# A Fourier layer's cosine transforms: cosines as the matmul's weights, in eighths of the array, with the modes turned by VectorE

## The chip, the cores and the metric

The kernel runs on one core of a Trainium2 chip. The metric is the device time of one execution in microseconds; the time before is the median of three runs. TensorE (PE) does the matmuls, VectorE (DVE), ScalarE (ACT) and GpSimd (POOL) the rest, and nearly all DMAs are issued from SyncE's queue (SP). PEld is TensorE's weight load, which overlaps its matmuls. PSUM has eight banks of 512 fp32 per partition here: four for attention (tag `pa`), four for the convolution (tag `pc`).

## What is computed

The input x is 32 images of 56 x 56 pixels with 128 channels, all fp32. Two residual layers follow each other:

```python
x = x + window_attention(group_norm(x))     # windows of 7 x 7, shifted by 3, 4 heads
x = x + fourier_block(group_norm(x))
```

The part that matters here is the second one. `N_MODES` is 32.

```python
def _forward_fourier(x, w0, w1):
    x = jnp.transpose(x, (0, 3, 1, 2))                      # b, channel, h, w
    x_fty = dct(x, norm='ortho', axis=-1)                   # along the width
    out_y = jnp.einsum('bixy,ioy->boxy', x_fty[..., :N_MODES], w0)
    xy = idct(out_y padded with zeros, norm='ortho', axis=-1)
    # the same along the height, with w1, gives xx
    return transpose_back(xx + xy)

def _feedforward(x, W1, b1, W2, b2):                        # 128 -> 512 -> 128
    return jax.nn.relu(x @ W1 + b1) @ W2 + b2
```

`fourier_block` is the feed-forward of `_forward_fourier`. So each line of 56 pixels becomes 32 cosine modes for each channel, each mode is mixed over the channels by its own 128 x 128 matrix, and the modes are turned back into 56 pixels.

## The kernel before

**Cycles.** The program goes through cycles; cycle n computes row n of windows (eight rows of windows per image, 256 in all). A row's attention is spread over several cycles: queries, keys and scores in its own cycle (`attn_qk`, L455 for the scores, L463 adds the bias, L473 takes the maximum), the exponential at its end, the division by the sum in the next (`attn_divide`, L499 on POOL), the transpose of the probabilities in the one after (`attn_transpose`, L509), then the values (`attn_values`, L524) and the projection (`attn_project`) three cycles later. L573 adds the residual to the projection and so makes the layer's output `x1`; L590 to L598 take its sums and squares for the next group norm.

**The convolution of an image** starts 11 cycles after its first row (`CONV_BEGIN`) and runs for 16 cycles, numbered c = 0 to 15, next to the attention of the images after. So the c = 8 to 15 of one image fall together with the c = 0 to 7 of the next, and "c = 2" below means both 2 and 10. In c = 0 the width is transformed, in c = 1 and 2 the height, in c = 3 the height's modes are mixed, in c = 4 and 5 the width's; the way back (`modes_back`, L743) is in c = 5 to 8, and the feed-forward in seven parts in c = 8, 9, 10, 12, 13, 14 and 15 (`ff_in`, L780, and `ff_out`, L815; its matmuls are recorded at L110, the helper `halved`).

**Order.** On PE, ACT, DVE and POOL the instructions are issued in the order in which the program is written: `halves_first`, then `eighths` (the values), `quarters` (the scores, and the way back), `attn_max`, `behind_max`, `halves_last`. The names tell what part of TensorE's array the matmuls use: halves are two tiles of 128 rows by 64 columns, quarters four of 64 by 64, eighths eight of 64 by 32. Each engine waits, in its own order, for what its next instruction needs.

**The transform** (`transform`, L670) takes two rows of pixels at a time: `tok` has 112 partitions (row parity r, then the 56 places) and 128 channels. The tokens are the weights, the cosines are the moving operand, block-diagonal for the two rows:

```python
py[hs, c * 2 * NM : (c + 1) * 2 * NM], lhsT=tok[:, c, hs], rhs=dct_sb     # L670: 64 channels by 64 columns
```

The result has the channels on the partitions, as the mixing needs. ScalarE copies it out (L678), scaled by the group norm's 1/std and reordered so that each mode's 56 lines lie side by side, and adds the shift to mode 0 (L685). For the width `tok` is `x1` in SBUF; for the height it is read back from a DRAM copy `scr` in the other order (`load_columns`, tile `htok`). The mixing (`mix`, L704) takes `y[:, k * S : k * S + JP]` as weights, 64 neighbouring numbers.

**Other names.** `load_tokens` and `chunks_of` load x again for the residual (tile `xr`), `add_bias` (L124) adds the projection's bias on POOL. `turn_quarter` (L312 to L323) and `row_stats` (L333) prepare the next image's attention. `load_back` fetches the mixed modes (tile `zT`), `load_quarter` the next image (tile `xin`).

Of the kernel before, what the change touches and what calls it, by code (L numbers as in the profile page):

```python
# [15 lines left out]
S = 56  # L16
# [20 lines left out]
HALVES = (slice(0, P // 2), slice(P // 2, P))  # L37
SQRT_S = float(np.sqrt(float(S)))
# [8 lines left out]
def swin_fourier_kernel(  # L47
# [41 lines left out]
    def chunks_of(t, b, n0, n1):  # L89

        tok = t[b].rearrange("h w c -> (h w) c")
        wrap = (S - SS) // 2
        if n0 < wrap:
            e = min(n1, wrap)
            part = tok[SS * S + n0 * TC : SS * S + e * TC].rearrange("(n p) c -> p n c", p=TC)
            yield n0, e, slice(0, TC), part
        if n0 <= wrap < n1:
            yield wrap, wrap + 1, slice(0, S), t[b, S - 1].unsqueeze(1)
            yield wrap, wrap + 1, slice(S, TC), t[b, 0].unsqueeze(1)
        if n1 > wrap + 1:  # L100
            a = max(n0, wrap + 1)
            t0 = (2 * a + SS) % S * S
            part = tok[t0 : t0 + (n1 - a) * TC].rearrange("(n p) c -> p n c", p=TC)
            yield a, n1, slice(0, TC), part
# [8 lines left out]
    def load_tokens(im, i):  # L113

        n0, n1 = WS * i // 2, WS * (i + 1) // 2
        t = work.tile([TC, 4, C], F32, tag="xr", name="xr", bufs=2)
        for a, e, p, src in chunks_of(x, im.b, n0, n1):
            nc.sync.dma_start(t[p, a - n0 : e - n0], src)
        im.xr[i] = t

    def add_bias(im, i):
        n = WS * (i + 1) // 2 - WS * i // 2
        piece = im.xr[i][:, :n]
        nc.gpsimd.tensor_tensor(  # L124
            piece, piece, bproj.unsqueeze(1).to_broadcast([TC, n, C]), ALU.add
        )

    HW = S // 2

    def load_quarter(b, k, u):  # L130

        if b:
            t = work.tile([P, HW, KB], F32, tag="xin", name="xin", bufs=1)
        elif u:
            t = others[k]
        else:
            t = big.tile([P, NM * S + JP - S], F32, tag="y", name="xin_first", bufs=2)
            t = t[:, : S * KB].rearrange("p (w c) -> p w c", w=S)
            others.append(t[:, HW:])
            t = t[:, :HW]  # L140
        rows = slice(k * (S - KB), k * (S - KB) + KB)
        for cb in range(C // KB):
            cs = slice(cb * KB, (cb + 1) * KB)
            queue = nc.scalar if b == 0 and cb % 2 else nc.sync
            queue.dma_start(t[cs], x[b, rows, u * HW : (u + 1) * HW, cs])
        return t
# [5 lines left out]
    x1 = big.tile([TC, NCH, C], F32, tag="x1", name="x1")  # L152
# [12 lines left out]
    bproj = const_load([TC, C], b_proj.partition_broadcast(TC), "bproj")  # L165
# [49 lines left out]
    dct_w = const_load([TC, 2 * NM], dct, "dct_w")  # L215
    dct_h = const.tile([TC, 2 * NM], F32, tag="dct_h", name="dct_h")
    for r in range(0, TC, S):
        nc.sync.dma_start(dct_h[r : r + S - SS], dct[r + SS : r + S])
        nc.sync.dma_start(dct_h[r + S - SS : r + S], dct[r : r + SS])
# [41 lines left out]
    gmean = const.tile([TC, P], F32, tag="gmean", name="gmean")  # L261
    nc.gpsimd.memset(gmean, 1.0 / (4 * NT))
# [29 lines left out]
    def image_begin(b):  # L292
        im = Image()
        im.b = b
        im.half, im.xw, im.xr, im.eT = {}, {}, {}, {}
        return im
# [215 lines left out]
    def attn_values(im, i, r):  # L512
# [19 lines left out]
        if i % 2 == 0:  # L532
            im.oT = work.tile([P, 2 * RT], F32, tag="oT", name="oT")
# [24 lines left out]
    def attn_project(im, i):  # L558

        if i == 0:  # L560
            im.scr = dram.tile([S, S, C], F32, tag="scr", name="scr", bufs=2)
        oT = im.oT
        n0, n1 = WS * i // 2, WS * (i + 1) // 2
        base = i // 2 * WS
        pp = attn_bank()
        for n in range(n0, n1):
            halved(
                pp[:TC, (n - n0) * C : (n - n0 + 1) * C],
                oT[:, (n - base) * TC : (n - base + 1) * TC],
                wproj,  # L570
            )
        piece = x1[:, n0:n1]
        nc.vector.tensor_tensor(  # L573
            piece,
            pp[:TC, : (n1 - n0) * C].rearrange("p (n c) -> p n c", c=C),
            im.xr[i][:, : n1 - n0],
            ALU.add,
        )
        nc.sync.dma_start(
            im.scr[2 * n0 : 2 * n1].rearrange("(n r) w c -> (r w) n c", r=2), piece  # L580
        )

    def attn_sums(im, i):

        n0, n1 = WS * i // 2, WS * (i + 1) // 2
        piece = x1[:, n0:n1]
        if i == 0:
            im.part = small.tile([TC, NWR, 2, C // 4], F32, tag="part", name="part", bufs=1)
            im.tot = small.tile([TC, 2, C // 4], F32, tag="tot", name="tot")
        nc.vector.tensor_reduce(  # L590
            im.part[:, i, 0],
            piece.rearrange("p n (g c) -> p g n c", c=4),
            axis=AX.XY,
            op=ALU.add,
        )
        sq = im.xr.pop(i)[:, : n1 - n0]
        nc.scalar.activation(sq, piece, AF.Square)  # L597
        nc.vector.tensor_reduce(  # L598
            im.part[:, i, 1],
            sq.rearrange("p n (g c) -> p g n c", c=4),  # L600
            axis=AX.XY,
            op=ALU.add,
        )


    def add_sums(im, i):
        if i:
            nc.gpsimd.tensor_tensor(
                im.tot, im.part[:, 0] if i == 1 else im.tot, im.part[:, i], ALU.add
            )  # L610

    def fourier_stats(im):
        pg = attn_bank()

        for k, t in enumerate((im.tot, im.part[:, NWR - 1])):
# [36 lines left out]
    def transform(im, width, g):  # L652

        if g == 0:
            y = big.tile([P, NM * S + JP - S], F32, tag="y", name="y", bufs=2)
            nc.gpsimd.memset(y[:, NM * S :], 0.0)
            if width:
                im.yw = y
            else:
                im.yh = y  # L660
        y = im.yw if width else im.yh
        if width:
            tok = x1[:, CH * g : CH * (g + 1)]
        else:
            tok = im.cols.pop(g)
        dct_sb = dct_w if width else dct_h
        py = conv_bank()
        for c in range(CH):
            for hs in HALVES:
                nc.tensor.matmul(  # L670
                    py[hs, c * 2 * NM : (c + 1) * 2 * NM],
                    lhsT=tok[:, c, hs],
                    rhs=dct_sb,
                    start=True,
                    stop=True,
                )
        y = y[:, : NM * S].rearrange("p (k s) -> p k s", s=S)
        nc.scalar.mul(  # L678
            y[:, :, 2 * CH * g : 2 * CH * (g + 1)].rearrange("p k (n r) -> p k n r", r=2),
            py[:, : 2 * CH * NM].rearrange("p (n k r) -> p k n r", k=NM, r=2),  # L680
            im.rstd,
        )
        if g == NCH // CH - 1:

            nc.scalar.activation(y[:, 0], y[:, 0], AF.Identity, bias=im.shift)  # L685

    def load_columns(im, g):

        t = work.tile([TC, CH, C], F32, tag="htok", name="htok", bufs=2)
        src = im.scr.rearrange("h (n r) c -> r h n c", r=2)  # L690
        for r in range(2):
            nc.sync.dma_start(t[r * S : (r + 1) * S], src[r, :, CH * g : CH * (g + 1)])
        im.cols[g] = t

    def mix(im, width, g):

        y, wmix = (im.yw, w0sb) if width else (im.yh, w1sb)
# [3 lines left out]
        for c in range(4):  # L701
            for u in range(2):
# [3 lines left out]
                    lhsT=y[:, k * S : k * S + JP],  # L706
# [229 lines left out]
    def half_columns(cycle, rest=False):  # L936
        for im, c in fourier(cycle):
            if rest and c != 3:
                continue
            if c == 0:  # L940
                next(im.stats, None)
                for g in range(4):
                    transform(im, True, g)
            elif c in (1, 2):
                for g in (2 * c - 2, 2 * c - 1):
                    transform(im, False, g)
                    if c == 1:
                        load_columns(im, g + 2)
# [3 lines left out]
            elif c in (4, 5):  # L952
                for g in (2 * c - 8, 2 * c - 7):
                    mix(im, True, g)

# [15 lines left out]
    def eighths(cycle):  # L971
        im, i = row(cycle - 3)
        if im:
            attn_values(im, i, cycle - 3)

# [8 lines left out]
    def next_steps(cycle):  # L984
# [4 lines left out]
            4: ((1, 0), (0, 1, 2)),  # L989
            5: ((1, 1), (3, 4, 5)),  # L990
# [16 lines left out]
    def halves_last(cycle):  # L1007
# [8 lines left out]
        load_first(cycle)  # L1016
        if cycle % NWR == NWR - 1:
            norm_step(cycle)
        if row(cycle)[0]:
            attn_exp(cycle)  # L1020
        im, j = row(cycle - 3)
# [58 lines left out]
    with tc.manual_schedule(engines={ET.PE, ET.Activation, ET.DVE, ET.Pool}):  # L1080
# [11 lines left out]
        extra = big.tile([P, NM * S + JP - S], F32, tag="y", name="a_extra", bufs=2)  # L1092
        extra = extra[:, : NH * NP * WT].rearrange("p (t w j) -> p t w j", t=NH, w=NP)
        a_sb.append(extra)
        for cycle in range(NB * NWR + CONV_BEGIN + FF_AT[-1] - NWR + 1):
# [4 lines left out]
            if not row(cycle - 3)[0]:  # L1100
                behind_max(cycle)
                half_columns(cycle)
                half_columns(cycle, True)
                load_first(cycle)
# [8 lines left out]
            if row(cycle)[0]:  # L1113
                attn_max(cycle)
            behind_max(cycle)
            halves_last(cycle)
# [62 lines left out]
```

## Time and profile before

| | before |
|---|---|
| median of 3 runs | 3375.59 us (3375.02 to 3377.16) |
| profiled execution, its own time | 3375.47 us |
| span of its profile | 3373.7 us |
| granted clock, mean | 0.991 |
| L670, width (`dct_w`): 3584 matmul records, mean | 117.7 us busy, 224 ns |
| L670, height (`dct_h`): 3584 matmul records, mean | 116.3 us busy, 222 ns |
| L704, mixing: 4096 matmul records | 124.9 + 122.8 us busy |
| L678, scaling on ACT: 256, mean | 167.5 us busy, 658 ns |

The page is one profiled execution. Busy times of one engine's groups can overlap on PE, where neighbouring tiles of the array run at the same time, so for PE the time from the start of one group to the start of the next tells more. Each fp32 matmul of the program leaves two records. The first number of a timeline row is its start in the span, the second its length in microseconds. "Idle before" is the engine's idle time, followed by what ended it; "issue" is idle time with no cause in the profile.

### The profile page before, as it was taken

To read this page: it belongs to the slowest core of one execution; us is meant where nothing else is said; L and a number is where in the kernel's file an instruction comes from. 1 tells how busy PE (TensorE), PEld (TensorE's weight loads), DVE (VectorE), ACT (ScalarE), POOL (GpSimd) and SP (SyncE) were. 2 spreads that over 40 slices of the span, in tenths; PEclk is the share of its full clock that TensorE was granted. 3 is DMA by queue.
4 is the path that set the end of the run, shared out by engine and by line. 5 is a ranking of instruction groups with operands and counts; after the bars stand their busy time and mean duration, and the time that the engine had idled before them with its cause. 6 is when DMAs were issued, how large, how long until landed. Compare 5 with 4: busy or idle time off the path is not lost.

```text
span 3373.7 us, 158286 instructions
## 1 busy us (share of the span) xinstructions
PE 3250.4 (96%) x69504; PEld 2559.6 (76%) x69504; DVE 2475.1 (73%) x4873; ACT 1979.3 (59%) x3649; POOL 2337.2 (69%) x2663
## 2 busy tenths in 40 slices
PE   4689999999999999999999999999999999999999
PEld 3567777777777777777787777777777777777776
DVE  7777777777777778777777777778777778777641
ACT  3456666555665566655666665666666666665553
POOL 6777777667767677777677676677777777677641
PEclk8899999999999999999999999999999999999999
DMA  5555555555555556556555555555555556555443
GB/s 101 115 128 137 141 137 137 128 132 141 136 132 134 131 140 148 134 132 140 134 140 143 130 131 135 134 137 138 139 133 137 136 137 149 132 133 138 110 130 100
DMA packets 1157657, 448.86 MB, mean 133 GB/s; under 512 B 509470, under 2 KB 1127104, under 8 KB 1156968
## 3 DMA queue, kind: packets, MB, share of 16 engines
q1 hardware_dynamic: 1148648, 437.34, 54.4%
q8 instruction: 546, 8.95, 1.2%
q10 hardware_dynamic: 7712, 1.24, 0.3%
q14 instruction: 143, 1.17, 0.1%
q0 software_dynamic: 608, 0.17, 0.0%
HBM read 277.01 MB, written 161.48 MB: 130 GB/s over the span
## 4 chain that ended last, share of the span: by engine, by line
PE 79%; DVE 7%; POOL 5%; ACT 4%; issue 3%; DMA 1%; SPq 0%; POOLq 0%; ACTq 0%; DVEq 0%
PE pc L110 36%; PE pa L110 13%; PE pa L433 6%; PE pc L670 5%; PE pc L743 5%; PE pa L455 5%; PE pa L524 4%; PE pc L704 4%; POOL blocks L499 4%; ACT hid L780 2%; POOL a L474 1%; DVE a L463 1%; DVE st L333 1%; DVE eT L509 1%; ACT k L420 1%
## 5 line engine op out<-in xcount | busy, mean ns | idle before, releaser
L499 POOL TENSOR_TENSOR blocks<-a,rs 128x512 f32<-128x512 f32 x1518 | 1289.2, 856 | 639.1 <-DVE rs L487 537.4
L110 PE MATMUL pc<-wff,hid 128*64 128x128 f32 x12544 | 744.2, 273 | 4.5 <-issue 3.2
L110 PE MATMUL pc<-xf,wff 128*64 128x512 f32 (+2 forms) x3584 | 720.2, 539 | 1.0 <-DVE xf L754 0.7
L110 PEld LDWEIGHTS pc<-wff,hid 128*64 128x64 f32 x12544 | 704.9, 137 | 13.3 <-issue 6.1
L110 PEld LDWEIGHTS pc<-xf,wff 128*64 128x64 f32 x3584 | 291.7, 136 | 343.7 <-issue 230.5
L474 POOL TENSOR_TENSOR a<-a,mx 128x784 f32<-128x784 f32 x253 | 381.5, 1508 | 241.8 <-DVE mx L473 208.6
L780 ACT ACTIVATE hid<-pc,b1sb 128x512 f32<-128x512 f32 (+2 forms) x896 | 513.0, 646 | 60.7 <-PE pc L110 52.3
L597 ACT ACTIVATE xr<-x 112x384 f32<-112x384 f32 (+1 forms) x256 | 147.1, 574 | 511.6 <-DVE x L573 511.6
L554 DVE TENSOR_SCALAR oT<-pa,bqkv 128x147 f32<-128x147 f32 (+2 forms) x768 | 171.0, 278 | 373.8 <-PE pa L524 373.8
L110 PE MATMUL pa<-xw,wn 128*64 128x392 f32 x2048 | 401.8, 501 | 29.0 <-ACT wn L389 28.8
L815 DVE TENSOR_TENSOR res<-pc,res 128x512 f32<-128x512 f32 (+3 forms) x257 | 142.9, 566 | 377.5 <-issue 169.5
L440 ACT COPY v<-pa 128x512 f32<-128x512 f32 x256 | 152.2, 595 | 366.0 <-PE pa L433 366.0
L787 POOL TENSOR_TENSOR res<-res,b2sb 128x512 f32<-128x512 f32 (+2 forms) x256 | 266.7, 1048 | 88.2 <-DMA res<-scr 88.1
L420 ACT ACTIVATE k<-pa,bqkv,heads 128x392 f32<-128x392 f32 x512 | 317.4, 673 | 1.6 <-PE pa L110 1.1
L509 DVE STREAM_TRANSPOSE eT<-blocks 128x1024 f32<-128x1024 f32 x256 | 315.6, 1233 | 1.6 <-POOL blocks L499 1.6
L124 POOL TENSOR_TENSOR xr<-xr,bproj 112x384 f32<-112x384 f32 (+1 forms) x256 | 292.3, 1142 | 14.9 <-DMA xr<-in_x_dram 14.7
L480 ACT ACTIVATE a<-a 128x784 f32<-128x784 f32 x253 | 216.2, 855 | 147.1 <-POOL a L474 146.2
L433 PE MATMUL pa<-wn,xw 128*64 128x128 f32 x4096 | 289.2, 282 | 12.0 <-issue 8.7
L463 DVE TENSOR_TENSOR a<-pa,bm 128x392 f32<-128x392 f32 x506 | 262.3, 560 | 35.8 <-PE pa L455 9.7
L524 PEld LDWEIGHTS pa<-eT,v 49*32 49x32 f32 x16384 | 173.3, 105 | 151.5 <-issue 97.0
L110 PE MATMUL pa<-wproj,oT 128*48 128x128 f32 (+1 forms) x3584 | 253.4, 276 | 18.5 <-DVE oT L554 17.3
L433 PEld LDWEIGHTS pa<-wn,xw 128*64 128x64 f32 x4096 | 225.1, 139 | 49.2 <-issue 11.1
(103 smaller groups left out, 5073.4 us busy)
## 6 DMA issues: line engine op xcount, KB each, us to landing
zscr<-z SPq DMA_DIRECT2D x512, 112.0 KB
xin<-in_x_dram SPq DMA_DIRECT2D x496, 112.0 KB
htok<-scr SPq DMA_DIRECT2D x256, 196.0 KB
zT<-zscr SPq DMA_DIRECT2D x192, 256.0 KB
res<-scr SPq DMA_DIRECT2D x160, 256.0 KB
out_dram<-res SPq DMA_DIRECT2D x160, 256.0 KB
scr<-x SPq DMA_DIRECT2D x128, 224.0 KB
xr<-in_x_dram SPq DMA_DIRECT2D x128, 168.0 KB
```

Source lines behind the costliest of these rows:

```text
L110: nc.tensor.matmul(dst[ps], lhsT=lhsT[:, ps], rhs=rhs, start=start, stop=stop)
L124: nc.gpsimd.tensor_tensor(piece, piece, bproj.unsqueeze(1).to_broadcast([TC, n, C]), ALU.add)
L420: nc.scalar.activation(k_sb[:, u], pk[:, :RT].rearrange("p (w j) -> p w j", j=WT), AF.Identity, bias=im.bias[:, 3 + u : 4 + u], scale=head ...
L433: nc.tensor.matmul(pv[HALVES[w % 2], w // 2 * C : (w // 2 + 1) * C], lhsT=im.half[i // NP][:, t0 : t0 + JP], rhs=im.w[:, 2 * C : 3 * C], s ...
L463: nc.vector.tensor_tensor(a[:, 2 * hp : 2 * hp + 2, :, 0:WT].rearrange("p u w j -> p w u j"), ps[hp][:, :RT].rearrange("p (w u j) -> p w u ...
L474: nc.gpsimd.tensor_tensor(a3, a3, mx.unsqueeze(2).to_broadcast([P, 2 * NWR, WT]), ALU.subtract)
L480: nc.scalar.activation(a2, a2, AF.Exp)
L499: nc.gpsimd.tensor_tensor(dst[to, k, :, :n], a3[src, :, kb * KB : kb * KB + n], rs[src].unsqueeze(2).to_broadcast([src.stop - src.start, 2 ...
L509: nc.vector.transpose(eT.rearrange("p t (k j) -> p k t j", k=2), blocks[r % 2])
L524: nc.tensor.matmul(po4[u][h * HD : (h + 1) * HD, pr], lhsT=v[ks, pr, h * HD : (h + 1) * HD], rhs=eT[ks, h * NP + pr, :WT], start=True, sto ...
L780: nc.scalar.activation(hf[:, :n], ph[:, :n], AF.Relu, bias=b1sb[:, f : f + 1])
L787: nc.gpsimd.tensor_tensor(im.res[:m, c0:c1], im.res[:m, c0:c1], b2sb[:m].unsqueeze(1).to_broadcast([m, c1 - c0, C]), ALU.add,)
```

## The change

The operands of the transform change places. The cosines become the weights (56 rows by 32 modes), the pixels the moving operand, and each matmul uses an eighth of the array: the two rows of a pair lie on partitions 0 to 55 and 64 to 119 (`LINE`), and four blocks of 32 channels go to four column blocks. The modes then come out on the partitions, 32 for each block of channels, and VectorE turns each 32 x 32 block on its way out of PSUM (`turn_modes`), which puts the channels on the partitions. ScalarE scales and shifts in SBUF, in place (`scale_modes`). `y` is one tile for both directions, in the order line, mode, so that the mixing's weights are 64 numbers with a step of 32.

```diff
+LINE = (slice(0, S), slice(JP, JP + S))
...
-    def transform(im, width, g):
...
-        for c in range(CH):
-            for hs in HALVES:
-                nc.tensor.matmul(
-                    py[hs, c * 2 * NM : (c + 1) * 2 * NM],
-                    lhsT=tok[:, c, hs],
-                    rhs=dct_sb,
...
-        nc.scalar.mul(
-            y[:, :, 2 * CH * g : 2 * CH * (g + 1)].rearrange("p k (n r) -> p k n r", r=2),
-            py[:, : 2 * CH * NM].rearrange("p (n k r) -> p k n r", k=NM, r=2),
-            im.rstd,
-        )
+    def transform(im, width, h):
+
         if width:
-            tok = x1[:, CH * g : CH * (g + 1)]
+            toks = [x1[:, 2 * CH * h : 2 * CH * (h + 1)]]
         else:
+            toks = [im.cols.pop(2 * h + j) for j in range(2)]
+        dct_sb = (dct_w if width else dct_h)[:, :, 0]
+        py = [conv_bank(), conv_bank()]
+        at = 0
+        for tok in toks:
+            n = tok.shape[1] * KB
+            for g in range(C // KB):
+                cs = slice(g * KB, (g + 1) * KB)
+                for r, ps in enumerate(LINE):
+                    nc.tensor.matmul(
+                        py[r][cs, at : at + n],
+                        lhsT=dct_sb[ps],
+                        rhs=tok[ps, :, cs],
+                        start=True,
+                        stop=True,
+                    )
+            at += n
+        im.py[width, h] = py
+
+    def turn_modes(im, width, h):
+
+        y = y_of[width].rearrange("p (h n r k) -> p h r n k", h=2, r=2, k=NM)[:, h]
+        for r, p in enumerate(im.py.pop((width, h))):
+            nc.vector.transpose(y[:, r], p[:, : 2 * CH * KB])
+
+    def scale_modes(im, width, h):
+
+        y = y_of[width].rearrange("p (h s k) -> p h s k", h=2, k=NM)[:, h]
+        nc.scalar.mul(y, y, im.rstd)
+        nc.scalar.activation(y[:, :, 0], y[:, :, 0], AF.Identity, bias=im.shift)
...
+        y = y_all[:, width * NM * S :][:, : NM * JP].rearrange("p (l k) -> p k l", k=NM)
...
-                    lhsT=y[:, k * S : k * S + JP],
+                    lhsT=y[:, k],
```

So that both rows start on partitions 0 and 64, `x1`, `xr`, `htok` and the projection's output get 128 partitions (8 of each 64 unused; the group norm's sums weigh them with 0), and the loads of `xr` and the stores to `scr` are issued for each row of a pair by itself:

```diff
-        nc.sync.dma_start(
-            im.scr[2 * n0 : 2 * n1].rearrange("(n r) w c -> (r w) n c", r=2), piece
-        )
+        dst = im.scr[2 * n0 : 2 * n1].rearrange("(n r) w c -> r w n c", r=2)
+        for r, ps in enumerate(LINE):
+            nc.sync.dma_start(dst[r], piece[ps])
```

Some steps move. The first half of the width's transform goes into c = 5 of the image before. The height's transforms go from the end of c = 1 and 2 to directly behind the values, in `eighths`; VectorE turns them behind `attn_max`, ahead of the transpose of the probabilities. The scaling follows `attn_exp`. The loads of `htok` are issued ahead of `halves_last`. Three of the next image's row statistics go from c = 1 and 2 (two and one) to c = 0:

```diff
             if c == 0:
                 next(im.stats, None)
-                for g in range(4):
-                    transform(im, True, g)
-            elif c in (1, 2):
-                for g in (2 * c - 2, 2 * c - 1):
-                    transform(im, False, g)
-                    if c == 1:
-                        load_columns(im, g + 2)
+                for h in range(int(im.b > 0), 2):
+                    transform(im, True, h)
+                    turn_modes(im, True, h)
...
+                if c == 5 and im.b + 1 < NB:
+                    transform(images[im.b + 1], True, 0)
+                    turn_modes(images[im.b + 1], True, 0)
...
+        for im, c in fourier(cycle):
+            if c == 1:
+                scale_modes(im, True, 1)
+            if c in (1, 2):
+                transform(im, False, c - 1)
+                if c == 1:
+                    for g in range(2):
+                        load_columns(im, g + 2)
+
+    def columns_turn(cycle):
+        for im, c in fourier(cycle):
+            if c in (1, 2):
+                turn_modes(im, False, c - 1)
+
+    def first_scale(cycle):
+        for im, c in fourier(cycle):
+            if c == 0:
+                scale_modes(im, True, 0)
+            elif c in (1, 2):
+                scale_modes(im, False, c - 1)
...
-            4: ((1, 0), (0, 1, 2)),
-            5: ((1, 1), (3, 4, 5)),
+            3: (None, (0, 1, 2)),
+            4: ((1, 0), (3,)),
+            5: ((1, 1), (4, 5)),
```

## The prediction

> **What bounds the kernel now.** I read the page first: its busy shares, then its chain by engine. Both name TensorE.
>
> ```profile
> PE 3250.4 (96%) x69504; PEld 2559.6 (76%) x69504; DVE 2475.1 (73%) x4873; ACT 1979.3 (59%) x3649; POOL 2337.2 (69%) x2663
> ...
> PE 79%; DVE 7%; POOL 5%; ACT 4%; issue 3%; DMA 1%; SPq 0%; POOLq 0%; ACTq 0%; DVEq 0%
> ```
>
> An average hides which cycle has room, so next came the table by stretches of one image in mid-run. A cycle is one row of windows; c is (cycle - 11) modulo 8. Each stretch runs from the attention values (L524) of a cycle to those of the next.
>
> ```profile
> 1342.60:1359.30 16.70, 16.43 (x376) 13.59 (x372) 10.28 (x22) 10.59 (x19) 11.05 (x13) 1.00 0.47 116
> 1359.30:1372.70 13.40, 13.40 (x273) 9.87 (x273) 10.50 (x20) 7.82 (x13) 8.75 (x11) 1.00 0.64 132
> 1372.70:1384.20 11.50, 11.50 (x293) 10.37 (x294) 10.14 (x19) 6.53 (x13) 7.79 (x9) 1.00 0.49 122
> 1384.20:1394.10 9.90, 9.90 (x186) 6.46 (x184) 8.29 (x17) 6.93 (x13) 8.49 (x11) 1.00 0.52 146
> ```
>
> These are c = 0 to 3: length, then busy time of PE, PEld, DVE, ACT and POOL, then the granted clock. PE fills each, at full clock. But in c = 2 VectorE works 10.14 of 11.50, and the change takes PE work out there and puts VectorE work in. So I followed c = 2 in order of time, by engine. The scores (L455) run on PE from 1373.44 to 1374.24; then VectorE:
>
> ```profile
> 1374.38 1.04 DVE L463 TENSOR_TENSOR a<-pa,bm 128x392 f32<-128x392 f32 x2
> 1375.45 0.97 DVE L473 TENSOR_REDUCE mx<-a 128x16 f32<-128x784 f32 x1
> 1376.34 1.23 DVE L509 STREAM_TRANSPOSE eT<-blocks 128x1024 f32<-128x1024 f32 x1
> 1377.50 1.09 DVE L312 STREAM_TRANSPOSE xw<-xin 128x512 f32<-128x512 f32 x1
> 1378.43 0.88 DVE L317 STREAM_TRANSPOSE xw<-xin 128x384 f32<-128x384 f32 x1
> 1379.17 0.26 DVE L323 COPY xw<-xw 128x168 f32<-128x168 f32 x1
> 1379.35 1.49 DVE L333 BATCH_NORM_STATS2 st<-xw 128x6 f32<-128x392 f32 x3
> 1380.76 0.66 DVE L815 TENSOR_TENSOR res<-pc,res 128x512 f32<-128x512 f32 x1
> 1381.35 0.54 DVE L573 TENSOR_TENSOR x<-pa,xr 112x384 f32<-112x384 f32 x1
> ```
>
> No pause from end to end. Then ScalarE, which stood idle 2.97 us for L573:
>
> ```profile
> 1381.92 0.52 ACT L597 ACTIVATE xr<-x 112x384 f32<-112x384 f32 x1 [2.97 <-DVE x L573]
> 1382.35 0.57 ACT L410 ACTIVATE q<-pa,bqkv 128x392 f32<-128x392 f32 x1
> 1382.82 1.24 ACT L420 ACTIVATE k<-pa,bqkv,heads 128x392 f32<-128x392 f32 x2
> ```
>
> k ends at 1384.06, and the next scores, which need it, start at 1384.90. So a second chain, VectorE to ScalarE to scores, lies 0.84 us under PE's. Over the trace's images k ends 0.85 us before the scores of c = 3 on average, 2.42 in c = 2, 2.67 in c = 1. That is all that PE can give up there.
>
> **The change part by part, for one image.**
>
> *PE, removed.* These are PE's rows in c = 2:
>
> ```profile
> 1375.20 1.80 PE L670 MATMUL pc<-dct_h,htok 112*64 112x64 f32 x56
> 1376.83 3.67 PE L110 MATMUL pc<-wff,hid 128*64 128x128 f32 x64
> ```
>
> From start to start 56 records take 1.63 us: 58.2 ns for two, which run side by side. L670's 7168 records are 112 such pairs an image: 6.52 us, 3.26 of it in c = 0, 1.63 in c = 1 and in c = 2.
>
> *PE, added.* The 64 records of L110 last to 1380.32: 109 ns a pair of 128 columns, 0.85 ns a column. L743 has four tiles side by side at that rate. The new form has eight (rows from 0 and 64, four column blocks). Its nearest row is L524, 49*32: 64 records in 0.74 us, and within that, eight records start in 44 ns, 0.9 ns a column; elsewhere in it they start more slowly, being short. With 448 or 224 columns eight records take 0.38 or 0.19 us. Width has 32 records an image, 1.51 us; height 64, 1.51; together 3.02. If four at once were the limit, 6.04. I take eight, by L524.
>
> *PE, changes of tile form.* From 64-row to 128-row tiles a step costs 0.1 us (L455's last record to L433's first 0.17, between L455's own sets 0.06). The height halves follow L524, which has their form: nothing. The width halves stand between 128-row groups, one in c = 0 and one in c = 5: four steps, 0.4.
>
> Relief: 6.52 - 3.02 - 0.4 = 3.1 us, 99 over 32 images.
>
> *VectorE, added.* Eight transposes of 128x448 out of PSUM. The rows on both sides:
>
> ```profile
> L509 DVE STREAM_TRANSPOSE eT<-blocks 128x1024 f32<-128x1024 f32 x256 | 315.6, 1233 | 1.6 <-POOL blocks L499 1.6
> ...
> L312 DVE STREAM_TRANSPOSE xw<-xin 128x512 f32<-128x512 f32 x124 | 137.0, 1105 | 0.7 <-DMA xin<-in_x_dram 0.7
> ```
>
> With L360 (32 columns, 212 ns), L509 gives 1.03 ns a column; it writes runs of 32. L312 scatters its columns 28 bytes apart: 1.83. The new ones write runs of 32: 0.64 us, of which some 0.08 lies beside the next instruction; two make 1.15 (by L312, 1.9).
>
> *VectorE, moved.* Three statistics (L333, 0.47 apart) go into c = 0, two out of c = 1, one out of c = 2. In c = 0 VectorE idles 4.12 us before L815; PE coming 2.3 earlier leaves 1.8 for 1.4 + 1.15, so L815 starts 0.75 late, out of the 2.67 of room in c = 1.
>
> *The wait in c = 3.* From the last score of c = 2 to k of c = 3 is 10.06 us on average, and becomes 10.06 + 1.15 - 0.47 = 10.75. PE reaches these scores after 10.90 now and after 10.90 - 1.63 = 9.27 then. Wait 1.5. On PE the scores, L433 and all that follows queue behind it.
>
> *The wait in c = 2.* The transform there now follows L524 and takes the two PSUM banks that this cycle's first two L780 free. k ends 10.28 + 1.15 - 0.93 = 10.50 after the scores of c = 1, the second L780 1.15 later, 11.65. PE is there at 10.95 (11.96 to L524 now, less 1.63, plus 0.62). Wait 0.7.
>
> *The wait in c = 0.* The width half wants two banks at once, those of the first two L754. The second ends at 1346.89; PE would come at 1346.5. Wait 0.4; today L670's first group covers it.
>
> *c = 5.* PE gets 0.95 more work, VectorE 1.15; k of c = 6 has 1.13 to spare: nothing.
>
> *The mixing weights.* L704's 64 columns come to lie 128 bytes apart. No strided weight load is in this trace. 32 columns load in 105 ns (L524), 64 in 137, so about 1 ns a column, 62 a load, under 109 for the pair of matmuls. By L312's 1.83 a load takes 113: 4 ns too long, 64 times, 0.25 us an image, 8 in all, which I take as the nearest strided row. Bounds: nothing, and, at a factor of 3, 186 ns, 4.9 us an image. [...]
>
> *ScalarE.* Eight L678 of 0.66 and two L685 go, 5.9 us; four scalings of 128x896 (0.95 by L480, 0.86 for 784) and four small ones of 0.3 come, 5.0. They stand before L597, in ScalarE's pause of 2.97. Nothing; without that pause 1.25 in c = 1 and c = 2.
>
> *DMA.* Stores to scr and loads of xr come in two halves, 17 more issues an image on SP at 0.3 to 0.57 us, 7 us over 101, where SP issues for 2.5 to 7.4 us of each 10 to 17. The loads of htok move ahead of zT's and xin's and wait for the last scr store alone. Nothing; a late xr would show as POOL idle at L124 (14.7 us now).
>
> *Gaps.* L670 has 14.8 us of idle time before its records, mostly "issue". Fewer, longer matmuls should lose half: -7 (0 to -15).
>
> Sum: -99 + 31 x (1.5 + 0.7 + 0.4) + 8 - 7 = -17 us. From the profiled execution's 3375.47 that is 3358.5; the median of the runs, 3375.59, stands 0.1 higher: 3358.6.
>
> **Rivals.**
> A: the second chain is not late, because it has slack I don't see. -99 - 7: 3269. Against it: VectorE's rows follow without a pause.
> B, slower: the turns cost what L312 costs, 0.75 more a pair, in the waits of c = 2 and c = 3: 46 us, 3405. For it: they read PSUM, which no transpose does now. It decides from 0.27 a pair (17 / 62).
> C, slower: strided weights at a third of the rate, (4.9 - 0.25) x 32 = 149, 3507. It decides from 0.8 us an image, a factor of 2.
> D: the eighths run four at once, so the change does not do what it says: 97 more, 3455.
>
> **How the numbers follow.** Forecast 0.50, its own range 3335 to 3380 (turns 0.15 a pair either way, 9; weights 0 to 16; gaps 0 to 15; no wait in c = 0, 12). A 0.13, B 0.17, C 0.08, D 0.06; waits in cycles taken as free 0.06, up to 3430. 3268 to 3430 leaves out C, D and a little more. 0.2%, 7 us, is what a measurement can tell: faster 0.38 + 0.13, same 0.09 + 0.01, slower the rest.
>
> **What would show it.** Right: 3072 records of the transform in some 97 us; the scores of c = 3 start right behind k, PE idle 1.5 us before them; 0.7 before the transform of c = 2. Wrong: PE busy 96% and no such idle time (A); turns near 1 us (B); L704's pairs well over 113 ns (C); a width half near 1.5 us (D).

## The result

The changed kernel takes 3404.6 us, the median of four runs (3401.19 to 3410.74); the kernel before took 3375.31 beside it. The ratio is 1.0088, 95% interval 1.0071 to 1.0106: slower by 0.9%, where 3358.6 was forecast. The time lies inside the wide range given (3268 to 3430) but outside the forecast's own (3335 to 3380), on the side that had a chance of 0.39. The profiled execution took 3401.19 us (span 3399.1, clock 0.987) against 3375.47 for the one before (clock 0.991), so the two traces differ by 25.7 us, and the forecast missed the profiled one by 42.7.

### The profile page after: what moved, and what is told of

Read it like the earlier page. It is cut to its first block, busy times and chain, and to the rows that moved or that the text cites. A ratio compares the mean times of both kernels' runs of the same rounds, so it can differ in the third digit from the quotient of the medians.

```text
span 3399.1 us, 150969 instructions
## 1 busy us (share of the span) xinstructions
PE 3242.7 (95%) x65408; PEld 2433.8 (72%) x65408; DVE 2624.2 (77%) x5129; ACT 1969.6 (58%) x3585; POOL 2335.6 (69%) x2609
## 5 line engine op out<-in xcount | busy, mean ns | idle before, releaser
L113 PEld LDWEIGHTS pc<-xf,wff 128*64 128x64 f32 x3584 | 275.6, 136 | 360.0 <-issue 240.4
L806 ACT ACTIVATE hid<-pc,b1sb 128x512 f32<-128x512 f32 (+2 forms) x896 | 504.9, 647 | 47.2 <-PE pc L113 46.0
L621 ACT ACTIVATE xr<-x,valid 128x384 f32<-128x384 f32 (+1 forms) x256 | 170.8, 667 | 447.0 <-DVE x L597 438.9
L453 PE MATMUL pa<-wn,xw 128*64 128x128 f32 x4096 | 296.8, 287 | 17.6 <-ACT oT L576 11.2
L127 POOL TENSOR_TENSOR xr<-xr,bproj 128x384 f32<-128x384 f32 (+1 forms) x256 | 292.7, 1143 | 10.5 <-DMA xr<-in_x_dram 10.2
L544 PEld LDWEIGHTS pa<-eT,v 49*32 49x32 f32 x16384 | 176.8, 105 | 161.0 <-issue 48.5
L475 PE MATMUL pa<-k,q 64*64 64x98 f32 x8192 | 238.3, 254 | 51.6 <-ACT k L440 51.0
L453 PEld LDWEIGHTS pa<-wn,xw 128*64 128x64 f32 x4096 | 231.4, 142 | 57.2 <-ACT oT L576 23.2
```

The lines of the kernel that those rows point to most:

```text
L113: nc.tensor.matmul(dst[ps], lhsT=lhsT[:, ps], rhs=rhs, start=start, stop=stop)
L127: nc.gpsimd.tensor_tensor(piece, piece, bproj.unsqueeze(1).to_broadcast([P, n, C]), ALU.add)
L453: nc.tensor.matmul(pv[HALVES[w % 2], w // 2 * C : (w // 2 + 1) * C], lhsT=im.half[i // NP][:, t0 : t0 + JP], rhs=im.w[:, 2 * C : 3 * C], s ...
L475: nc.tensor.matmul(ps[hp][HALVES[e], pr * 2 * WT : (pr + 1) * 2 * WT], lhsT=q[cs, w * WT : w * WT + JP], rhs=k_sb[cs, :, w], start=True, s ...
L544: nc.tensor.matmul(po4[u][h * HD : (h + 1) * HD, pr], lhsT=v[ks, pr, h * HD : (h + 1) * HD], rhs=eT[ks, h * NP + pr, :WT], start=True, sto ...
L806: nc.scalar.activation(hf[:, :n], ph[:, :n], AF.Relu, bias=b1sb[:, f : f + 1])
```

## The profile after

The page's busy shares:

```profile
PE 3242.7 (95%) x65408; PEld 2433.8 (72%) x65408; DVE 2624.2 (77%) x5129; ACT 1969.6 (58%) x3585; POOL 2335.6 (69%) x2609
```

PE's records fell by 4096, but its busy time by only 7.7 us: 99 were forecast to go from its work. Something on PE grew. The table by stretches of one image, c = 0 to 3 as before (length, busy time of PE, PEld, DVE, ACT, POOL, clock, DMA):

```profile
1348.47:1362.80 14.33, 14.33 (x281) 9.45 (x277) 12.67 (x27) 8.53 (x16) 10.38 (x12) 1.00 0.52 136
1362.80:1375.46 12.66, 12.66 (x250) 8.85 (x248) 10.48 (x20) 7.89 (x14) 7.92 (x9) 1.00 0.62 141
1375.46:1386.84 11.38, 11.38 (x263) 9.65 (x261) 9.04 (x16) 5.28 (x9) 8.20 (x9) 1.00 0.34 89
1386.84:1399.28 12.44, 10.57 (x187) 6.82 (x185) 10.51 (x22) 9.31 (x17) 9.52 (x11) 1.00 0.47 144
```

The stretch of c = 0 is 2.4 us shorter and that of c = 1 0.7, as PE's relief would have it; c = 3 is 2.5 longer and PE stands idle 1.87 us in it. The chain that the prediction followed is there, in VectorE's order of c = 2:

```profile
1380.39 1.17 DVE L704 STREAM_TRANSPOSE y<-pc 128x448 f32<-128x448 f32 x2
...
1384.27 0.72 DVE L343 COPY xw<-xw 128x168 f32<-128x168 f32 x1
1384.91 1.02 DVE L353 BATCH_NORM_STATS2 st<-xw 128x6 f32<-128x392 f32 x2
```

The two turns take 1.17 us, where 1.15 was forecast. The copy L343 takes 0.72, where it took 0.26. It runs beside an instruction of GpSimd and ends 0.10 us behind it; the same copy of the kernel before ended 0.10 us behind L787, which it met only near that one's end. GpSimd's two instructions, after and before:

```profile
1383.60 1.29 POOL L127 TENSOR_TENSOR xr<-xr,bproj 128x512 f32<-128x512 f32 x1
```

```profile
1378.02 1.29 POOL L787 TENSOR_TENSOR res<-res,b2sb 128x512 f32<-128x512 f32 x1
```

ScalarE comes next, in order of time:

```profile
1387.03 0.61 ACT L621 ACTIVATE xr<-x,valid 128x384 f32<-128x384 f32 x1 [2.70 <-DVE x L597]
1387.55 0.57 ACT L430 ACTIVATE q<-pa,bqkv 128x392 f32<-128x392 f32 x1
1388.02 1.24 ACT L440 ACTIVATE k<-pa,bqkv,heads 128x392 f32<-128x392 f32 x2
1389.15 1.07 ACT L738 COPY z<-pc 128x512 f32<-128x512 f32 x2
1390.09 0.47 ACT L576 ACTIVATE oT<-pa,bqkv 128x196 f32<-128x196 f32 x1
```

And PE, which waits first for k and then for L576, which frees the bank that the v product L453 writes:

```profile
1389.31 0.90 PE L475 MATMUL pa<-k,q 64*64 64x98 f32 x32 [1.47 <-ACT k L440]
1390.62 1.09 PE L453 MATMUL pa<-wn,xw 128*64 128x128 f32 x16 [0.40 <-ACT oT L576]
```

Over the whole span PE's waits for k ahead of the scores (us, times, longest) are these, after and before:

```profile
PE pa L475 <- ACT k L440: 51.0, 39, 1.7
```

```profile
PE pa L455 <- ACT k L420: 7.9, 8, 1.7
```

Two more things are in this trace. The first is the load of a mixing weight: row by line and shape, busy us and mean ns, of the kernel after and then of the kernel before.

```profile
L730 PEld LDWEIGHTS pc<-w0sb,y 128*64 128x64 f32 x2048 | 135.1, 218 | 1.6 <-issue 1.4
```

```profile
L704 PEld LDWEIGHTS pc<-w0sb,y 128*64 128x64 f32 x2048 | 115.9, 138 | 2.0 <-issue 1.6 <-ACT hid L780 0.3
```

The second is the clock. Cut into stretches at the clock's own changes, in another image of the trace (the last values: clock, DMA share, GB/s):

```profile
1488.13:1491.54 3.41, 1.94 (x92) 1.60 (x92) 3.34 (x9) 2.61 (x6) 1.33 (x2) 1.00 0.47 133
1491.54:1494.96 3.42, 3.42 (x52) 3.13 (x46) 2.38 (x4) 1.35 (x4) 3.17 (x5) 0.50 0.49 153
1494.96:1498.40 3.44, 3.44 (x50) 2.88 (x48) 2.41 (x5) 2.10 (x4) 3.33 (x4) 1.00 0.34 117
```

In the first row PE works 1.94 us of 3.41: the wait for k lies in it. In the next 3.41 us the granted clock is 0.50, and then it is full again. Such a stretch costs some 1.7 us where PE is at work throughout, an estimate from its clock and its length; here the 32 records of the scores take 1.32 us and L453's 16 take 1.97, where the rows above have 0.90 and 1.09. Between 215 and 3300 us of the span the trace has 9 such stretches, all beginning within 1.7 us of the start of the scores of c = 3; the trace before has none. Each of the 9 is 3.413 us long, and they begin whole multiples of that apart (30, 60, 360, 390 and so on after the first), so a window below is one of these lengths of 3.413 us.

To add up where the 25.7 us came from, I took the time from the first record of each group of matmuls to the first record of the next, by line, in both traces. The transform went from 231.7 to 152.0 (-80). The mixing went from 229.2 to 267.0 (+38). The values L544, which hold the wait for k, went from 200.3 to 246.7, and the scores, which hold the wait for L576, from 231.1 to 238.1 (+53 together). L453, which takes most of the halved clock, went from 256.7 to 264.8 (+8). The products of x with `wn` gained 7, in no single place, and the rest comes to nothing. That makes 26.

## The experiments

Two theories stood at the start. One: strided mixing weights cost what the rows show, 1.2 us an image, and k is late in c = 3 through VectorE's queue. The other: the mixing is longer because of waits, and k is only the last of several late things. Each ratio below is to the kernel before, run beside it on the same chip, with a 95% interval.

### The weights: a_packed and b_strided

```diff
# a_packed, from the changed kernel
-                    lhsT=y[:, k],
+                    lhsT=y_all[:, width * NM * S + k * S :][:, :JP],
# b_strided, from the kernel before
-                    lhsT=y[:, k * S : k * S + JP],
+                    lhsT=y[:, : JP * 28].rearrange("p (l k) -> p k l", k=28)[:, k % 28],
```

> The changed kernel, but the mixing multiplications (L730) take 64 adjacent numbers as weights, as the kernel before does, instead of 64 numbers 128 bytes apart; the mixing then works on the wrong numbers. All else stays. Theory (the strided weights cost PE 1.2 us an image: 130 ns a pair of matmuls against 112 in the two traces): a pair goes back to 112 ns, a load record from 218 to about 137 ns. Eight groups an image, of which the first two of c = 3 lie ahead of the wait for k and only lengthen that wait, so six of eight count: 1.2 x 6/8 x 32 = 28 us less, 3376 (3368 to 3382). Rival (the price in the prediction, 0.25 us an image, is right and PE's longer mixing comes from waits for the z copies on ScalarE): at most 8 us less, 3397 or more.

> The kernel before, but the mixing multiplications (L704) take 64 numbers 112 bytes apart as weights instead of 64 adjacent ones (112, not 128, so that they fit the buffer there); the mixing then works on the wrong numbers. Theory (strided weights alone cost 1.2 us an image, whatever else changes): all eight groups are on PE's path here, and k has 0.85 us to spare, so 38 us more, 3413 (3405 to 3420). Rival (strided weights cost 0.25 us an image as predicted): 8 us more, 3383.

a_packed: 3393.57 us, 1.0054 (1.0041 to 1.0066). b_strided: 3387.07, 1.0033 (1.0021 to 1.0044). Both missed the theory and came near the rivals: 11 us less by the ratios, where 28 were expected, and 13 more, where 38 were. The records say why. In a_packed a load is back at 138 ns and the w0sb groups at 116.7 us (132.5 after, 114.0 before), so 16 us went from this half of the mixing alone. In b_strided a load takes 204 ns and the mixing 245.4 us, 16 more than before: twice the rival's price, but not half of the theory's. Its step is 112 bytes and not 128, which is cheaper (203 ns a load and not 217 in the table under a_steps). What ate a_packed's gain is in its clock:

```profile
core 0: 3391.5 us, clock 0.979
```

Between 215 and 3300 us it has 23 stretches at 0.50, at the estimated 1.7 us each 39 us, against 9 stretches and 15 us in the changed kernel. Their starts (1492.87, 1595.27, 1697.67 us) lie 102.4 us apart, which is one image and 30 windows of 3.413 us: each image's wait meets the same part of a window.

### The order on ScalarE: a_qk_first and b_qk_first

```diff
     (halves_first; the same in both kernels)
+        im, i = row(cycle)
+        if im:
+            attn_qk(im, i)
         if last and cycle > CONV_BEGIN:
             attn_sums(last, j)
         next_tokens(cycle)
-        im, i = row(cycle)
-        if im:
-            attn_qk(im, i)
```

> The changed kernel, but ScalarE copies q and k (L430, L440) before it squares x (L621), not behind it: attn_qk is called before attn_sums in halves_first. Theory (the idle time of PE in c = 3, 51.6 us before the scores and 11.2 before L453, comes from k standing behind the Square, which waits for VectorE's x): k then ends right behind PE's own products, the wait before the scores goes. But L576, behind the Square and two z copies on ScalarE, still ends at about 1389.1 of the trace's image, 0.5 us after the scores would end, so L453 starts 1.5 us earlier than now and not 2.0: 31 x 1.5 = 46 us less, 3358 (3345 to 3368), with PE's idle time before L453 at 15 to 20 us. Rival (PE is late for another reason, such as eT or the banks, and k is only the last of several): less than 15 us less.

> The kernel before with the same exchange of attn_qk and attn_sums, as a control. Theory: k is 0.85 us early in c = 3 and 2.4 or more elsewhere, so there is nothing to gain: within 5 us of the time before. Rival (the exchange helps by itself, whatever the change did): 20 us less or more.

a_qk_first: 3391.26 us, 1.0049 (1.0035 to 1.0063), 13 us less where 46 were expected. b_qk_first: 1.0002 (0.9993 to 1.0011), as expected. The wait for k went (from the last score of c = 2 to the first of c = 3 it is 9.42 us, after 11.15, both medians), but a new one came in c = 4. PE's waits (us, times, longest):

```profile
PE pa L453 <- ACT oT L576: 64.8, 58, 2.0
```

Of these 50.6 us lie in c = 4 and 14.2 in c = 3; in the changed kernel they were 1.7 and 9.5.

The sums L505 and L507 still stand behind VectorE's queue of c = 2, GpSimd's divide starts behind them, its next subtraction behind that, and the exponential, q, k, the Square and four relus on ScalarE come after it and ahead of L576. So k is only the first of two chains that VectorE makes late in c = 2, and taking k out of it moved the wait.

### Filling the wait: a_busy, a_packed_busy and a_packed_fill

```diff
# a_busy, a_packed_busy (attn_values)
+        again = 3 if i == 3 and r >= CONV_BEGIN - 3 else 1
-        for pr in range(NP):
+        for pr in [p for _ in range(again) for p in range(NP)]:
# a_packed_fill (attn_values, ahead of the loop as it was)
+        if i == 3 and r >= CONV_BEGIN - 3:
+            for _ in range(3):
+                halved(po[0], wff1[:, :P], wff1)
```

> The changed kernel, but PE issues the attention values (L544) of c = 3 three times over, into the same banks, so that it works for 1.5 us more where it now stands idle before the scores of c = 3; the result stays as it is. Theory (each stretch of 1.5 us or more of idle PE makes the granted clock fall to 0.50 for 3.41 us, 1.7 us lost each time, some 13 to 22 us a run more than in the kernel before): PE's idle time before L475 goes, the clock stays at 1.00 in mid-run (mean 0.990), k comes no later, and the time falls by 13 to 22 us although PE does more work: 3386 (3380 to 3394). Rival (the idle time has nothing to do with the clock, or the extra work delays what follows): 3404 or more.

> The kernel a_packed (mixing weights as 64 adjacent numbers, the mixing on the wrong numbers), with the values of c = 3 issued three times over as in a_busy. Theory: a_packed loses 41 us more than the kernel before to a clock of 0.50, since its images take 102.4 us, 30 windows of 3.41 us, and its idle stretch falls at the same place of a window each time; with no idle stretch the clock goes back to 0.990 and the time to 3353 (3347 to 3364). Rival: 3390 or more.

Both missed: 3446.53 us, 1.0235 (1.0218 to 1.0252), and 3419.83, 1.0158 (1.0144 to 1.0172). The fill did not work as a fill:

```profile
PE pa L545 <- issue: 38.0, 20, 2.8
```

In 20 places of a_busy PE stands still inside these short records, up to 2.8 us, with nothing to wait for that the profile shows. Between 215 and 3300 us a_busy has 12 stretches of halved clock and a_packed_busy 16. Why PE stands still is open; it spoils the test. Hence the third, with six long matmuls:

> The kernel a_packed (mixing weights as 64 adjacent numbers, the mixing on the wrong numbers), with six matmuls of 512 columns (some 1.35 us of PE work) ahead of the values of c = 3, into a bank that the values then write over. a_busy filled the idle stretch with 128 records of 12 ns and PE then stood still inside these records, up to 2.8 us at a time, with nothing to wait for that the profile shows; six long matmuls can't run into that. Theory (1.5 us or more of idle PE in a window of 3.41 us halves the granted clock in the next window): no idle stretch before L475, no clock of 0.50 in mid-run, and 41 us less than a_packed although PE does 40 us more work: 0.988 of a_packed's time (0.985 to 0.992). Rival (the halved clock in a_packed comes from something other than idle time, or idle time is no loss): a_packed's time or more.

3371.16 us, 0.9999 (0.9990 to 1.0008): 0.5% under a_packed's 1.0054, although PE does 83 us more work. The 1.35 us expected was half of what the fill takes: a matmul of fp32 leaves two records, so six leave twelve, of 224 ns. No stretch at 0.50 is left between 215 and 3300 us, and the clock is back:

```profile
core 0: 3369.7 us, clock 0.991
```

That is 0.994 of a_packed's time by the ratios, not the 0.988 expected. The fill of 2.7 us is longer than the wait and delays the scores of c = 3 by 0.6 us (12.40 us from scores to scores, after 11.81 in a_packed), 18 us over 31 images; from there to the scores of c = 4 it is 9.95 us on average, after 11.42. The 39 us of a_packed's clock less these 18 make 21, where the ratios show 18. So idle time of PE brought a_packed's 23 stretches of halved clock, and work put in its place took them away.

### VectorE's queue: a_stats, b_stats, a_packed_stats and a_stats_copy

```diff
# a_stats (next_steps); a_packed_stats is a_packed with it
-            5: ((1, 1), (4, 5)),
-            6: (None, (6, 7)),
+            5: ((1, 1), ()),
+            6: (None, (4, 5, 6, 7)),
# a_stats_copy, on top of a_stats
-                nc.vector.tensor_copy(b[:, :, KB:], a[:, :, :SS])
+                if im.b > 1:
+                    im.edge = b[:, :, KB:], a[:, :, :SS]
+                else:
+                    nc.vector.tensor_copy(b[:, :, KB:], a[:, :, :SS])
...
         first_scale(cycle)
+        b, quarter, _ = next_steps(cycle)
+        if quarter == (1, 1) and b > 1:
+            nc.scalar.copy(*images[b].edge)
```

b_stats makes the same move of rows 4 and 5 in the kernel before.

> The changed kernel, but the two BN statistics (L353) of c = 2, rows 4 and 5, are done in c = 3, with rows 6 and 7. Theory (VectorE's queue in c = 2 makes k of c = 3 late): x, the Square and k come 1.0 us earlier, the wait before the scores of c = 3 falls from 1.5 to about 0.5 and that before L453 from 0.4 to 0; L505 and with it GpSimd's divide come earlier too, so nothing new is late in c = 4; and without a long idle stretch the clock stays full. 31 x 1.0 to 1.4 plus 13 to 22 us: 3352 (3340 to 3362). Rival (as in a_qk_first the wait only moves, to L453 of c = 4, since x of c = 3 now stands behind four statistics): 3385 to 3404.

> a_packed and a_stats together (the mixing on the wrong numbers). Theory (strided weights cost 0.25 us for each of the four groups of a half image's mixing, 32 us a run by the w0sb rows, and the wait and the clock are apart from that): without the waits all eight groups count, so 20 to 32 us under a_stats: 3326 (3310 to 3342). Rival (strided weights cost 8 to 13 us, as a_packed and b_strided seem to say by their totals): within 15 us of a_stats.

> a_stats, and the copy of the edge columns (L343 there, 0.72 us of VectorE in c = 2, against 0.31 in the kernel before) is done by ScalarE at the end of c = 2, behind first_scale, where it waits 2.70 us for x. Theory (what is left of the wait of c = 3, 28.7 us, is VectorE's queue in c = 2): x and k 0.7 us earlier, 31 x 0.7 = 22 us under a_stats, 0.990 of the kernel before (0.987 to 0.994). Rival (PE, not k, is next and VectorE's queue no longer counts): as a_stats, 0.997.

> The kernel before, with the two BN statistics of rows 4 and 5 done in c = 3 and not in c = 2: a control for a_stats. Theory (k is 0.85 us early there, VectorE's queue in c = 2 costs nothing yet): the time before, 0.998 to 1.002. Rival (that move is a gain by itself, and a_stats owes the turned transform nothing): 0.990.

a_stats: 3356.40 us, 0.9968 (0.9955 to 0.9980), faster than the kernel before, near what the theory said. k comes 0.94 us earlier (10.16 us behind the last score of c = 2, after 11.10, both medians), and the wait for k halves:

```profile
PE pa L475 <- ACT k L440: 28.7, 38, 1.7
```

The changed kernel has the 51.0 shown above. The clock has no stretch at 0.50 in mid-run. a_packed_stats: 3337.66, 0.9917 (0.9905 to 0.9929), 17 us under a_stats by the ratios, less than the 20 to 32 expected, and nearly the rival's. Its trace says why: PE reaches the wait for k sooner, and waits there and before L453 61 us in all, 20 more than in a_stats. Packing is worth more than it shows while k is late. It also says something of the clock: PE's idle time between 200 and 3200 us is 63 us there and 74 in a_packed, much the same, but no window of 3.41 us holds more than 1.4 us of it, where a_packed has up to 1.87, and the clock stays full.

a_stats_copy: 3339.63, 0.9910 (0.9896 to 0.9923), 0.6% under a_stats as expected. The copy takes 0.32 us on ScalarE, and no wait for k of 0.15 us or more is left in c = 3, though the scores still start right behind k (0.05 us); what is left lies in single cycles, most of them the first:

```profile
PE pa L478 <- ACT k L443: 8.1, 8, 1.7
```

b_stats: 3387.28, 1.0052 (1.0039 to 1.0065), slower, which neither theory expected. There k gains only 0.15 us in c = 3 (L815, ahead of x in VectorE's queue, now waits 0.7 us for PE's L110 in the image that I followed), x in c = 3 comes 0.9 us later, and PE waits up to 0.7 us before L433 of c = 4 for L556 (20.0 us in all). So the move is no gain by itself: it pays only where VectorE's queue in c = 2 is the late one.

### Turning into contiguous weights: a_modes

```diff
# on top of a_stats_copy
-        y = y_of[width].rearrange("p (h n r k) -> p h r n k", h=2, r=2, k=NM)[:, h]
+        y = y_of[width].rearrange("p (k h n r) -> p h r n k", h=2, r=2, k=NM)[:, h]
...
-                    lhsT=y[:, k],
+                    lhsT=y_all[:, width * NM * S + k * S :][:, :JP],
```

> a_stats_copy, and the turns (L704 there) write each mode's 56 numbers side by side, 224 bytes between columns of a block, so that the mixing takes 64 adjacent numbers as weights; the scaling reads and writes that form. The result is that of the reference. Theory A (a scattered transpose costs what L332 does, 1.83 ns a column against 1.38 here, so 0.2 to 0.36 us a turn more): the mixing wins 32 us, k of c = 3 loses up to 0.7 us (22 us): 0.987 of the kernel before (0.981 to 0.993). Theory B (the scatter costs nothing): 0.981. Theory C (at 224 bytes it costs twice): 0.997 or more.

3358.48 us, 0.9963 (0.9950 to 0.9977): 19 us above a_stats_copy, near theory C's time, with theory A's cause. A turn takes 1016 ns, not 622 (0.39 more, a little above A's 0.36, not C's double), c = 2 is 0.6 us longer from scores to scores, and PE's waits before the scores and before the v product come back to 59 us, nearly what the changed kernel has (62). Scattering moved the price from PE, which had it outside the wait, to the queue that makes k late.

### What sets the price of a strided load: a_steps and a_pad

```diff
# a_steps, on top of a_stats_copy
+        step = ((1, 4, 16, 28), (32, 33, 36, 40))[width][g]
-                    lhsT=y[:, k],
+                    lhsT=y_all[:, : 64 * step : step],
# a_pad, on top of a_stats_copy: NR = NM + 1 numbers in a row of y_all, the last unused
```

> a_stats_copy, with another step between the 64 numbers of a mixing weight in each of the eight groups of an image, in 4-byte numbers: 1, 4, 16, 28 (the groups of w1sb), 32, 33, 36, 40 (those of w0sb). The mixing works on the wrong numbers. Read from the load records and from the start of one pair of matmuls to the next. [...] Theory C (it grows with the step): 16 lies between 1 and 28, 40 above 32.

> a_stats_copy, with the turned modes in rows of 33 numbers instead of 32, the last one unused, so that a mixing weight's 64 numbers lie 132 bytes apart and not 128. The result is that of the reference. Theory (the step alone sets the price: 7 ns less for each of 64 pairs an image and width half, 64 x 7 x 32 = 14 us, of which the part ahead of the wait of c = 3 may not count): 10 to 14 us under a_stats_copy, 0.987 to 0.988 of the kernel before. Rival (PE stands in the same waits, or the turns into rows of 33 cost more): 0.990 or more.

Medians over the 32 images of a_steps, from its load and matmul records (a pair is two matmul records side by side, from start to start):

| step, bytes | 4 | 16 | 64 | 112 | 128 | 132 | 144 | 160 |
|---|---|---|---|---|---|---|---|---|
| load record, ns | 137 | 209 | 217 | 203 | 217 | 207 | 212 | 272 |
| pair, ns | 109 | 120 | 126 | 117 | 126 | 119 | 120 | 160 |

A load takes 209 ns at 16 bytes, where adjacent numbers take 137, and 203 to 217 from there to 144: the price comes at once at 16 bytes, the shortest step that was run, and up to 144 a longer one hardly adds to it. So theory C falls in the main: 64 bytes (step 16), at 217 ns, does not lie between 137 and 203, though 160 (step 40) lies above 128. Nor is it one price: 112 and 132 bytes, at 117 and 119 ns a pair, are cheaper than 64 and 128, at 126, and 160 bytes costs a pair 51 ns over 4 bytes, three to six times as much as the rest, for which no run has a cause. (The single run took 3350.75 us, beside 3375.92.) a_pad's pairs take 118 ns as the table says, its turns stay at 622, and its time is 3339.88, 0.9895 (0.9877 to 0.9913): under a_stats_copy by less than the runs can tell, and short of the 10 to 14 us expected. Part of it went into waits, as the rival had it: PE stands 31 us before its scores and its v product, after 22 in a_stats_copy.

So the best version here is a_stats_copy or a_pad, about 1% under the kernel before, and both compute the same result as it.

## Why the prediction was wrong, by its own steps

**Right: what PE loses and gains in the transform.** Eighths do run eight at once (eight records of 224 columns in 0.19 us), so rival D falls; PE's idle time before the scores of c = 3 does the same for rival A. With the waits for a second bank in c = 0 and c = 2, which show as first records that run alone, the four halves take 1.45 (c = 0), 1.04, 1.40 and 0.91 us, 4.8 an image where the steps add to 4.5. The trace has -80 us for the transform; relief, these waits and the gaps were -72. The wait in c = 2 is 0.36 (1.40 against 1.04 in c = 1) and not 0.7; in c = 0 it is 0.53 and not 0.4.

**Right: the turns.** 622 ns against 0.64. Rival B's 3405 is the time that came, but by accident: its condition, turns near 1 us, isn't met. a_modes meets it, at 1016 ns, and lost 19 us net of what its packed weights gained, so B's price was of the right size, though no run measured it by itself.

**Right in kind, too small: the wait in c = 3.** k was forecast 10.75 us behind the scores of c = 2 and came at 11.10. Of the 0.35, the copy of 0.72 us instead of 0.26 is more than all. PE is idle 1.47 us there, as forecast (1.5), since its longer mixing fills the difference. Not forecast was the second wait behind it, 0.40 before L453: ScalarE's two z copies and L576 stand behind the late k as well. The term was 46 us and the phases show 53, some 3 of them from the clock.

**Wrong: the mixing weights, the largest error of the sum.** The term was 8 us, at 113 ns a pair, taken from VectorE's scattered write (L312) as the nearest strided row; the mixing measured +38, with pairs at 126 ns, where the forecast's own range allowed 0 to 16. Some 4 of the 38 come from the clock. This is rival C's mechanism at 17 ns a pair and not 77, and past the point that C named: it decides from 0.8 us an image, and it was 1.2. VectorE's write was no measure for PE's load here: the estimate adds 51 ns to a load (62 to 113), and the records grew by 80 at 128 bytes, by 66 at 112 and by 135 at 160. In the forecast's sum this term alone turns the sign (-17 + 30). In the measured kernel it is not alone: a_packed, without the strided weights, is still slower than the kernel before, because of its clock, and a_stats, with them, is faster.

**Missing: the clock.** No step priced what 1.5 us of idle time did to PE's clock behind it. It was 15 us in the profiled run by its 9 stretches, at the estimated 1.7 us each: 7 in L453, 4 in the mixing, 3 in the scores. The other three runs of the changed kernel had a clock of 0.983 to 0.984 and took 1.7 to 9.6 us longer. In six of the 9 windows ahead of a stretch PE was idle for 1.47 us, in the others for 1.68 and 1.87.

The mixing's 38 and the waits' 53 hold 7 of the clock's 15, so 8 are left to add. The forecast's own sum then comes to -17 + 30 + 7 + 8 - 8 = +20 us over the kernel before (weights, waits of c = 3, clock, transform), and to +27 with the 7 of the products of x, which no step priced and whose cause stays open; 25.7 is what the two profiled executions differ by.

## What to carry to other kernels

Where a change takes work from the bound engine, price what it does to that engine's operands by a row of the same engine, or carry the whole span between the bounds: 64 weights with a step of 128 bytes cost PE 17 ns a pair of matmuls here (126 against 109), and 8 to 51 at the steps of a_steps. Where the gain turns into waiting, look for what else stands in the late engine's queue: moving two statistics and a copy, some 1.7 us in all, out of the cycle whose VectorE queue makes k late made a slowdown of 0.9% into a gain of 0.9%, and the same move of the statistics in the kernel before was a loss. Reordering the consumer, as in a_qk_first, mostly moved the wait, since another chain left the same queue.

## What the runs showed of the hardware

- In mid-run PE's granted clock fell to 0.50 for one window of 3.41 us behind a window in which PE stood idle for about 1.5 us (9 times in the changed kernel, 23 in a_packed). It is not a sharp bound. In these two the windows ahead of a halved one have 1.47 to 1.87 us of idle time, and one in a_modes has 1.38. But seven windows of the same two kernels with 1.41 to 1.69 kept the full clock, as did all of a_packed_stats, with up to 1.4, and most of those with 1.7 in a_qk_first. What else counts is open. In a_packed an image takes 102.4 us, 30 windows, and the three starts shown lie just that far apart.
- 64 fp32 weights load in 203 to 217 ns at the six steps run from 16 to 144 bytes (a_steps), in 137 where they are adjacent, and at 160 bytes in 272.
- VectorE's copy L343 takes 0.72 us where a GpSimd TENSOR_TENSOR (L127) runs beside it, and 0.24 in the one instance in the same trace with GpSimd at rest. In the other 31 of its 32 instances, and in all 32 of the same copy in the kernel before (0.23 to 0.96 us long), it ends 0.10 to 0.11 us behind an instruction of GpSimd, whichever that is. Why is open: no run moved one against the other alone.
- A transpose of 128x448 out of PSUM takes 622 ns with runs of 32 numbers and 1016 ns with single numbers 224 bytes apart; with rows of 33 numbers, the last unused, it stays at 622 (a_pad).
